# Attention's products and the combination ordered by matmul shape, and routing's small VectorE steps traced as three runs

## The chip, the cores and the metric

The kernel runs on one core of one Trainium2 chip. The metric is the device time of one execution in microseconds (us); lower is better. Three runs of the kernel before took 4184.38, 4184.52 and 4186.29 us, so its median is 4184.52 us. The engines are named as in the profile: PE is TensorE (PEld its weight loads), DVE is VectorE, ACT is ScalarE, POOL is GpSimd, and SP is the engine whose queue issues most of the DMAs.

## What is computed

The input x holds 4 images of 384 channels and 32 x 32 points, in fp32. Everything stays in fp32. Cut to what matters:

```python
# layer 0: a selective scan (a state space model) over 4 directions
dt = softplus(dts + bias); h = h * exp(dt * A) + (dt * u) * B; y = sum over 16 states of h * C
x  = x + gelu(layernorm(y0 + y1 + y2 + y3))
# layer 1: attention in a window, then a mixture of experts
t = tokens(x)                                   # per image 1024 tokens of 384
q, k, v = split(ln(t) @ qkv_w + qkv_b)          # 6 heads of 64
att = where(causal and distance <= 64, q @ k.T / 8, -inf)
t = t + (softmax(att) @ v) * gate @ proj_w + proj_b
probs = softmax(ln(t) @ gate_w + gate_b)        # 4 experts, the best 2 of them kept
t = t + sum over the 2 experts of weight * (gelu(ln(t) @ w1[e] + b1[e]) @ w2[e] + b2[e])
```

Because a token attends to itself and to at most 64 tokens before it, a tile of 128 tokens needs the 128 keys of its own and the last 64 of the tile before. The first tile of an image needs its own alone.

## The kernel before

**The order of the work** is not written by hand. Every stage is a Python generator that yields one operation at a time, and a planner, `Machine` (L211), keeps a clock for each engine. It knows an estimated cost for each operation (`Engine.ask`, L154) and takes from the waiting operations the one that can start first, corrected by a bias (`EARLY`, -6, for what feeds others; `LATER`, +6, for the experts and the combination). The order in which the planner takes the operations is the order in which each engine executes them, and the engines then wait for each other by semaphores alone. So an estimate of a cost changes no work, but it can change the order everywhere behind it. `Engine.all` (L143) takes a list of calls as one operation: they stand together in the engine's order, and nothing is placed among them. The planner also decides which of two engines does certain steps: `copy` (L557) gives a copy to DVE or ACT, and `scan` gives the multiplication by C to POOL or DVE (`on_pool`, L853).

**The scan.** The work is cut into 768 slots: 4 images, 4 directions, 12 blocks and 4 groups of states. For each slot ACT makes the decays `dA`, POOL multiplies `z <- dts, bc` (`times_b`, L804), DVE runs the scan over 1024 steps (`scan`, L846), then DVE or POOL multiplies by C, and PE folds the states together (`fold_y`, L876, the tile `ps_y`). Seven buffers `z` are in use. A fold gives its two back, so a fold that is late on PE can hold up POOL.

**Attention** (`tokens`, L953) starts for an image when its scan is done, while the scan of the next image goes on. It takes the image in 8 tiles of 128 tokens, up to three of them in progress, with one at a time in the core of attention. For each tile it does the following steps on PE, with copies and sums on the other engines between them:
- It makes q and k by 9 matmuls each (`ps_qk`). The keys of a head pair lie in 192 columns of the tile `k`: 64 old ones first, then the 128 new ones. A copy brings the old ones from the tile before.
- It makes v (`ps_v`).
- It makes the scores (`ps_s`, L1061). One matmul for each head has 64 rows, which are the head's channels, and 192 columns. DVE adds the mask and finds the maximum, and ACT takes the exponential with its sum.
- It turns the probabilities (`ps_p`, L1094), for three pairs of heads. For each head there is a transpose of the 128 new columns and, in tiles with old keys, a matmul by the identity that turns the 64 old columns onto partitions 64 to 127. Its weights have 64 columns.
- It multiplies by v (`ps_o`, L1115). For each head there is a matmul over 128 rows, the new keys, and in tiles with old keys one over 64 rows, which adds to it. The two kinds alternate. DVE then scales the result by the sums (`o <- ps_o, sums`).
- It projects (`ps_pr`), normalises, and finds the logits of the experts (`ps_xt`, with 4 columns).

**Routing** (`route`, L1196) computes for the 1024 tokens of an image the weights of the two experts and the place of each token in the lists of the experts. These are some 65 DVE steps on small tiles, with one exponential on ACT and three small matmuls on PE among them. Each step is yielded on its own. Then the tokens are scattered in DRAM by indirect DMAs.

**The experts** (`experts`, L1304) take 19 blocks of 128 tokens for each image. A block needs 36 hidden matmuls (`ps_hid`, 128 columns) and 12 output matmuls (`y_ff`, 384 columns), and 8 loads of 576 KB of weights. The experts of one image follow its routing, and PE does them between the folds and the attention of the images after it.

**The combination** (`combine`, L1396) gathers for each tile of 128 tokens the outputs of its two experts, weighs and adds them (ACT, then DVE), and turns the sum with matmuls by the identity. Onto each of three column groups it adds the biases `b2`, by a matmul over 4 rows (`ps_c`, L1421). These two kinds alternate too.

A fp32 matmul is two instructions on PE in the profile, one for each pass, and a transpose is one.

Of the kernel before, what the change touches and what calls it, by code (L numbers as in the profile page):

```python
# [17 lines left out]
P = 128  # L18
# [111 lines left out]
class Engine:  # L130
# [23 lines left out]
    def ask(self, op, a, k):  # L154
# [222 lines left out]
def conv_attn_hybrid(  # L377
# [11 lines left out]
    def const_load(src, shape, name):  # L389
# [57 lines left out]
    nc.gpsimd.affine_select(  # L447
        mask, mask, pattern=[[1, KW]], compare_op=ALU.is_ge, fill=NEG,
        base=0, channel_multiplier=-1,
# [503 lines left out]
    def tokens(b):  # L953
# [18 lines left out]
        def tile(a):  # L972
# [32 lines left out]
            for n, (w, dst) in enumerate(  # L1005
                ((wq, q[:, :D].rearrange("p (t l) -> p t l", t=T)), (wk, kv[:, :, WIN:]))
            ):
# [39 lines left out]

            lo = 0 if a else WIN
            yield lambda: len(core) < CORES
# [5 lines left out]
            def score(hps, j):  # L1055
# [3 lines left out]
                for n, hp in enumerate(hps):  # L1059
                    mm.matmul(  # L1060
                        ps[:, n * KW + lo : (n + 1) * KW],  # L1061
                        q[r, ts(hp, P)], k[r, hp * KW + lo : (hp + 1) * KW],
                        start=True, stop=True,
                    )
                yield from pe.all(mm)
                for n, hp in enumerate(hps):
                    h = 2 * hp + j
                    c = slice(n * KW + lo, (n + 1) * KW)
                    yield from dve.tensor_tensor_reduce(
                        s[hps[0] + j][:, c], ps[:, c], mask[:, lo:], 1.0, NEG,  # L1070
                        ALU.add, ALU.max, mx[:, 0, h : h + 1],
# [7 lines left out]
            for hp in range(T):  # L1079
                for j in range(2):  # L1080
                    h = 2 * hp + j
                    sj = s[hp // 2 * 2 + j][:, hp % 2 * KW + lo : (hp % 2 + 1) * KW]
                    yield from act.activation(
# [6 lines left out]
            def turn(hp):  # L1090
# [105 lines left out]
    def route(b):  # L1196
# [22 lines left out]
        yield from dve.reciprocal(r, rr)  # L1219
        yield from dve.tensor_tensor(pp, pp, bcast_last(r, NE), ALU.mult)  # L1220
        yield from dve.tensor_copy(p, pp)

        yield from dve.memset(cmp, 0.0)
        for e in range(NE):
            if e > 0:
                yield from dve.tensor_tensor(
                    cmp[:, :, e, :e], p[:, :, :e], bcast_last(pp[:, :, e], e), ALU.is_ge
                )
            if e < NE - 1:
                yield from dve.tensor_tensor(  # L1230
                    cmp[:, :, e, e + 1 :], p[:, :, e + 1 :], bcast_last(pp[:, :, e], NE - 1 - e),
                    ALU.is_gt,
                )
        sel = rp.tile([P, NT, NE], F32, tag="sel", name="sel2", bufs=1)
        yield from dve.tensor_reduce(rank, cmp, AX.X, ALU.add)
        yield from dve.tensor_scalar(sel, rank, 2.0, None, ALU.is_lt)
        yield from dve.tensor_tensor(pp, pp, sel, ALU.mult)
        yield from dve.tensor_reduce(rr, pp, AX.X, ALU.add)
        yield from dve.tensor_scalar(rr, rr, 1e-9, None, ALU.add)
        yield from dve.reciprocal(r, rr)  # L1240
        yield from dve.tensor_tensor(p, pp, bcast_last(r, NE), ALU.mult)

        accs = rp.tile([P, NT + 1, NE], F32, tag="acc", name="acc", bufs=1)
        yield from dve.memset(acc[:, 0, :], 0.0)
        for a in range(NT):
            yield from dve.tensor_tensor(acc[:, a + 1, :], acc[:, a, :], sel[:, a, :], ALU.add)
        yield from dve.tensor_copy(accs, acc)
# [4 lines left out]
        yield from pe.all(mm)  # L1254
        nb = rp.tile([P, NE], F32, tag="nb", name="nb")
        yield from dve.tensor_tensor(full, bcast_last(cn[:, NT, :], NT), bcast(count_p, NE), ALU.is_gt)
        yield from dve.tensor_reduce(nb, full, AX.X, ALU.add)

        yield from dve.tensor_copy(cum[:, :1], nb[:, :1])
        for e in range(1, NE):  # L1260
            yield from dve.tensor_tensor(
                cum[:, e : e + 1], cum[:, e - 1 : e], nb[:, e : e + 1], ALU.add
            )
        yield from dve.tensor_tensor(nb, cum, nb, ALU.subtract)
        slot = rp.tile([P, NT, NE], F32, tag="slot", name="slot", bufs=1)
        yield from dve.scalar_tensor_tensor(
            slot, bcast(nb, NT), float(P), cn[:, :NT, :], ALU.mult, ALU.add
        )

        eid = rp.tile([P, MB], mybir.dt.int32, tag="eid", name="eid")  # L1270
        yield from dve.tensor_tensor(
            past, bcast_last(count, NE - 1), bcast(cum[:, : NE - 1], MB), ALU.is_ge
        )
        yield from dve.tensor_reduce(eid_f, past, AX.X, ALU.add)
        yield from dve.tensor_copy(eid, eid_f)

# [3 lines left out]
        for n, far in enumerate((65536.0, -65536.0)):  # L1280
            yield from dve.tensor_scalar(big, sel, -far, far, ALU.mult, ALU.add)
            yield from dve.tensor_tensor(big, big, slot, ALU.add)
            yield from dve.tensor_reduce(place[:, n, :], big, AX.X, ALU.max if n else ALU.min)
            yield from dve.tensor_tensor(big, big, bcast_last(place[:, n, :], NE), ALU.is_equal)
            yield from dve.tensor_tensor(big, big, p, ALU.mult)
            yield from dve.tensor_reduce(gate[:, n, :], big, AX.X, ALU.add)
        yield from dve.tensor_copy(idx, place)
        banks.give(ps)
# [107 lines left out]
    def combine(b):  # L1396
# [3 lines left out]
        def one(a):  # L1400
# [115 lines left out]
```

## Time and profile before

| | |
|---|---|
| median of 3 runs | 4184.52 us (4184.38 to 4186.29) |
| the profiled execution | 4192.68 us, of which its span is 4190.3 us |
| mean granted TensorE clock | 0.796 |
| busy: PE / DVE / POOL / ACT | 3169.3 / 2882.8 / 2844.5 / 2403.3 us |
| product with v, `ps_o` | 720 passes, 128 rows: 342 ns mean, 64 rows: 359 ns mean |
| turned probabilities, `ps_p` | 192 transposes and 336 passes, 104.9 us busy |
| combination, `ps_c` | 384 passes, 97.8 us busy |
| last fold of the scan / start of the last combination | about 3231 us / about 4131 us |

The profile is one execution. Busy times are sums over an engine's instructions, and they say little on their own: what counts is which engine the others wait for in a stage. [...] The granted clock is the share of full speed that the throttle allows TensorE. It is 1.0 or 0.5 at any moment, and a mean in a table.

### The profile page before, as it was taken

The numbers are of one execution on the slowest core, as the hardware profiler recorded it, in microseconds if no ns is written. First come the engines' busy times: TensorE is split into PE (matmuls) and PEld (weight loads), VectorE is DVE, ScalarE is ACT, GpSimd is POOL, SyncE is SP. The second block draws the span as 40 slices with busy tenths as digits, with TensorE's granted clock in tenths as the row PEclk, the third lists the DMA queues.
The fourth block names the chain that finished last, engine by engine and source line by source line (L and its number), as shares of the span: only waits on it lengthen the run. The fifth ranks groups of instructions, "written<-read, shape, count | busy, mean of one in ns | idle before, by whom it ended". The sixth has DMA issues, their size and how long they took to land. (4 is left out here: it accounts for less than half of the span.)

```text
span 4190.3 us, 49613 instructions
## 1 busy us (share of the span) xinstructions
PE 3169.3 (76%) x16030; PEld 1930.3 (46%) x16030; DVE 2882.8 (69%) x3068; ACT 2403.3 (57%) x3952; POOL 2844.5 (68%) x1484
## 2 busy tenths in 40 slices
PE   3454454477774797777888776878899999999997
PEld 1000000044541464444545443444467788787885
DVE  2999999988888888888778899888876222201001
ACT  3555465566664788877677777776677343322221
POOL 1999889988887898989876898999887011011001
PEclk8555565577765898887779887877799999999997
DMA  5566564534346989554569875554589555798995
GB/s 202 204 232 229 190 232 139 182 108 157 103 148 211 341 303 340 187 192 147 165 222 328 307 276 205 198 189 147 185 277 345 191 185 167 247 355 298 312 317 164
DMA packets 368572, 935.12 MB, mean 223 GB/s; under 512 B 48373, under 2 KB 160121, under 8 KB 368313
## 3 DMA queue, kind: packets, MB, share of 16 engines
q1 hardware_dynamic: 360120, 906.79, 62.4%
q0 software_dynamic: 8192, 25.17, 1.7%
q8 instruction: 127, 2.08, 0.2%
q14 instruction: 133, 1.08, 0.1%
HBM read 786.39 MB, written 164.30 MB: 227 GB/s over the span
## 5 line engine op out<-in xcount | busy, mean ns | idle before, releaser
L141 POOL TENSOR_TENSOR z<-dts,bc 128x1024 f32<-128x1024 f32 x768 | 1791.4, 2357 | 233.8 <-PE ps_y L152 155.8
L152 PE MATMUL ps_y<-z,fold 128*32 128x512 f32 x3072 | 732.7, 800 | 531.3 <-POOL z L141 269.2
L141 ACT ACTIVATE dA<-dts,a 128x1024 f32<-128x1024 f32 x768 | 850.7, 1115 | 493.8 <-DVE z L141 485.7
L141 DVE TENSOR_TENSOR_SCAN dA<-dA,z 128x1024 f32<-128x1024 f32 x398 | 910.5, 2288 | 101.5 <-ACT dA L141 94.0
L141 POOL TENSOR_TENSOR z<-z,bc 128x1024 f32<-128x1024 f32 x370 | 867.4, 2355 | 128.6 <-DVE z L141 118.7
L141 DVE TENSOR_TENSOR_SCAN z<-dA,z 128x1024 f32<-128x1024 f32 x370 | 832.0, 2276 | 25.5 <-ACT dA L141 24.3
L152 PEld LDWEIGHTS ps_hid<-xbt,w_sb 128*128 128x128 f32 x5472 | 688.7, 203 | 137.0 <-issue 32.3
L152 PE MATMUL ps_hid<-xbt,w_sb 128*128 128x128 f32 x5472 | 710.5, 288 | 44.1 <-ACT dt L141 17.5
L152 PE MATMUL y_ff<-w_sb,hs 128*128 128x384 f32 x1824 | 663.8, 502 | 16.4 <-ACT hs L141 8.1
L141 ACT ACTIVATE hs<-ps_hid,bb 128x128 f32<-128x128 f32 x912 | 271.2, 367 | 486.5 <-PE ps_hid L152 390.9
L152 PEld LDWEIGHTS ps_y<-z,fold 128*32 128x32 f32 x3072 | 93.6, 123 | 953.0 <-POOL z L141 461.8
L141 DVE TENSOR_TENSOR z<-dA,bc 128x1024 f32<-128x1024 f32 x398 | 486.1, 1221 | 12.9
L141 ACT ACT_TABLE_LOAD x368 | 472.1, 1283 | 22.7 <-PE ps_g L152 7.7
L152 PEld LDWEIGHTS y_ff<-w_sb,hs 128*128 128x128 f32 x1824 | 330.9, 194 | 237.8 <-issue 42.9
L141 POOL DMA_INDIRECT cb<-ysdr,idx x64 | 61.8, 966 | 499.2 <-DMA cb<-t2dr 265.4
L141 DVE COPY xbt<-ps_xb 128x384 f32<-128x384 f32 x36 | 20.0, 557 | 384.4 <-PE ps_xb L152 384.3
L152 POOL TENSOR_TENSOR rn<-rn,half 128x1 f32<-128x1 f32 x96 | 52.4, 546 | 279.4 <-DVE rn L152 273.7
L152 PE MATMUL ps_o<-v,pt 128*128 128x64 f32 x720 | 163.0, 350 | 18.5 <-DVE tt L141 6.5
L141 POOL DMA_INDIRECT xsdr<-tks,idx x64 | 64.1, 1001 | 152.2 <-DMA xsdr<-tks,idx 97.2
L152 PEld LDWEIGHTS ps_o<-v,pt 128*128 128x128 f32 x720 | 133.0, 233 | 57.8 <-ACT dt L141 8.2
L152 PE MATMUL ps_p<-ident,s 128*128 128x128 f32 (+1 forms) x528 | 104.9, 328 | 47.7 <-ACT dt L141 21.1
L152 PE MATMUL ps_dt<-xd,dtw_sb 12*128 12x512 f32 x192 | 97.5, 858 | 43.9 <-ACT dt L141 19.4
(188 smaller groups left out, 3314.7 us busy)
## 6 DMA issues: line engine op xcount, KB each, us to landing
w_sb<-wl SPq DMA_DIRECT2D x608, 576.0 KB
dts<-dtr SPq DMA_DIRECT2D x384, 512.0 KB
bc<-xdr SPq DMA_DIRECT2D x128, 512.0 KB
ub<-udr SPq DMA_DIRECT2D x48, 512.0 KB
dtr<-e SPq DMA_DIRECT2D x48, 512.0 KB
dtr<-dt SPq DMA_DIRECT2D x48, 512.0 KB
yp<-ydr SPq DMA_DIRECT2D x96, 256.0 KB
ydr<-yp SPq DMA_DIRECT2D x96, 256.0 KB
```

Source lines behind the costliest of these rows:

```text
L141: return getattr(self.real, op)(*a, **k)
L152: getattr(self.real, op)(*a, **k)
```

## The change

There are four parts.

1. The keys are laid out with the 128 new ones first and the 64 old ones behind. Masks, copies and slices follow. The mask is built by three selections on POOL instead of two.
2. The turned probabilities come from transposes alone. The old keys are turned by a transpose of the last 128 columns (64 new, 64 old) of the 192, of which partitions 64 to 127 are used.
3. In the product with v all heads' 128-row matmuls come first, then all 64-row ones. One accumulation covers the bank: the first matmul starts it, and the last ends it. The combination does the same with its identity matmuls and its 4-row ones.
4. Routing's DVE steps are handed to the planner as three lists, one up to the exponential, one up to the matmuls and one behind them, instead of one by one. And the planner's estimate of a matmul has a floor of 122 columns instead of 90.

```diff
-            cost = max(n, 90) * (0.00088 if op == "transpose" else 0.00176)
+            cost = max(n, 122) * (0.00088 if op == "transpose" else 0.00176)
...
     nc.gpsimd.affine_select(
-        mask, mask, pattern=[[-1, KW]], compare_op=ALU.is_ge, fill=NEG,
-        base=WIN, channel_multiplier=1,
+        mask[:, :P], mask[:, :P], pattern=[[-1, P]], compare_op=ALU.is_ge, fill=NEG,
+        base=0, channel_multiplier=1,
     )
...
-                yield from copy(kv[:, :, :WIN], old.rearrange("p (t l) -> p t l", t=T)[:, :, P:])
+                yield from copy(kv[:, :, P:], old.rearrange("p (t l) -> p t l", t=T)[:, :, P - WIN : P])
...
                 for j in range(2):
-                    mm.transpose(ps[:, ts(j, P)], s[base + j][:, c0 + WIN : c0 + KW], ident)
+                    mm.transpose(ps[:, ts(j, P)], s[base + j][:, c0 : c0 + P], ident)
                 for j in range(2 if a else 0):
-                    mm.matmul(
-                        ps[WIN:, ts(2 + j, P)], s[base + j][:, c0 : c0 + WIN], ident,
-                        start=True, stop=True,
-                    )
+                    mm.transpose(ps[:, ts(2 + j, P)], s[base + j][:, c0 + KW - P : c0 + KW], ident)
...
-            for hp, pt in sorted(pts.items()):
-                for j in range(2):
-                    hc = slice((2 * hp + j) * HD, (2 * hp + j + 1) * HD)
-                    mm.matmul(po[:, hc], pt[:, ts(j, P)], v[:, hc], start=True, stop=not a)
-                    if a:
-                        mm.matmul(
-                            po[:, hc], pt[WIN:, ts(2 + j, P)], vts[a - 1][WIN:, hc],
-                            start=False, stop=True,
-                        )
+            for old in (False, True) if a else (False,):
+                for hp, pt in sorted(pts.items()):
+                    for j in range(2):
+                        hc = slice((2 * hp + j) * HD, (2 * hp + j + 1) * HD)
+                        if old:
+                            lhs, rhs = pt[WIN:, ts(2 + j, P)], vts[a - 1][WIN:, hc]
+                        else:
+                            lhs, rhs = pt[:, ts(j, P)], v[:, hc]
+                        last = len(mm) == (2 if a else 1) * HEADS - 1
+                        mm.matmul(po[:, hc], lhs, rhs, start=not mm, stop=last)
...
-        yield from dve.tensor_reduce(r, p, AX.X, ALU.max)
-        yield from dve.tensor_tensor(pp, p, bcast_last(r, NE), ALU.subtract)
+        mm = Calls()
+        mm.tensor_reduce(r, p, AX.X, ALU.max)
+        mm.tensor_tensor(pp, p, bcast_last(r, NE), ALU.subtract)
+        yield from dve.all(mm)
         yield from act.activation(pp, pp, AF.Exp)
-        yield from dve.tensor_reduce(rr, pp, AX.X, ALU.add)
+        mm = Calls()
+        mm.tensor_reduce(rr, pp, AX.X, ALU.add)
...
             for t in range(T):
                 c = ts(t, P)
-                mm.matmul(ps[:, c], gs[0][:, c], ident, start=True, stop=False)
-                mm.matmul(ps[:, c], b2_sb[:, c], gt[:NE, :P], start=False, stop=True)
+                mm.matmul(ps[:, c], gs[0][:, c], ident, start=t == 0, stop=False)
+            for t in range(T):
+                c = ts(t, P)
+                mm.matmul(ps[:, c], b2_sb[:, c], gt[:NE, :P], start=False, stop=t == T - 1)
```

More of the change, by code (lines that the diff above doesn't have):

```diff
@@ L443, in conv_attn_hybrid @@
     nc.gpsimd.affine_select(
-        mask, mask, pattern=[[-1, KW]], compare_op=ALU.is_ge, fill=NEG,
-        base=WIN, channel_multiplier=1,
+        mask[:, :P], mask[:, :P], pattern=[[-1, P]], compare_op=ALU.is_ge, fill=NEG,
+        base=0, channel_multiplier=1,
     )
     nc.gpsimd.affine_select(
-        mask, mask, pattern=[[1, KW]], compare_op=ALU.is_ge, fill=NEG,
+        mask[:, :P], mask[:, :P], pattern=[[1, P]], compare_op=ALU.is_ge, fill=NEG,
+        base=WIN, channel_multiplier=-1,
+    )
+    nc.gpsimd.affine_select(
+        mask[:, P:], mask[:, P:], pattern=[[1, WIN]], compare_op=ALU.is_ge, fill=NEG,
         base=0, channel_multiplier=-1,
@@ L1005, in tile @@
             for n, (w, dst) in enumerate(
-                ((wq, q[:, :D].rearrange("p (t l) -> p t l", t=T)), (wk, kv[:, :, WIN:]))
+                ((wq, q[:, :D].rearrange("p (t l) -> p t l", t=T)), (wk, kv[:, :, :P]))
             ):
@@ L1046, in tile @@
             vts[a] = v
-            lo = 0 if a else WIN
+            n_keys = KW if a else P
             yield lambda: len(core) < CORES
@@ L1060, in score @@
                     mm.matmul(
-                        ps[:, n * KW + lo : (n + 1) * KW],
-                        q[r, ts(hp, P)], k[r, hp * KW + lo : (hp + 1) * KW],
+                        ps[:, n * KW : n * KW + n_keys],
+                        q[r, ts(hp, P)], k[r, hp * KW : hp * KW + n_keys],
                         start=True, stop=True,
@@ L1067, in score @@
                     h = 2 * hp + j
-                    c = slice(n * KW + lo, (n + 1) * KW)
+                    c = slice(n * KW, n * KW + n_keys)
                     yield from dve.tensor_tensor_reduce(
-                        s[hps[0] + j][:, c], ps[:, c], mask[:, lo:], 1.0, NEG,
+                        s[hps[0] + j][:, c], ps[:, c], mask[:, :n_keys], 1.0, NEG,
                         ALU.add, ALU.max, mx[:, 0, h : h + 1],
@@ L1081, in tile @@
                     h = 2 * hp + j
-                    sj = s[hp // 2 * 2 + j][:, hp % 2 * KW + lo : (hp % 2 + 1) * KW]
+                    sj = s[hp // 2 * 2 + j][:, hp % 2 * KW : hp % 2 * KW + n_keys]
                     yield from act.activation(
@@ L1214, in route @@
         r = rp.tile([P, NT], F32, tag="r", name="r")
-        yield from dve.tensor_reduce(r, p, AX.X, ALU.max)
-        yield from dve.tensor_tensor(pp, p, bcast_last(r, NE), ALU.subtract)
+        mm = Calls()
+        mm.tensor_reduce(r, p, AX.X, ALU.max)
+        mm.tensor_tensor(pp, p, bcast_last(r, NE), ALU.subtract)
+        yield from dve.all(mm)
         yield from act.activation(pp, pp, AF.Exp)
-        yield from dve.tensor_reduce(rr, pp, AX.X, ALU.add)
[L1219 to L1223, printed above, removed]
+        mm = Calls()
+        mm.tensor_reduce(rr, pp, AX.X, ALU.add)
+        mm.reciprocal(r, rr)
+        mm.tensor_tensor(pp, pp, bcast_last(r, NE), ALU.mult)
+        mm.tensor_copy(p, pp)
+        mm.memset(cmp, 0.0)
         for e in range(NE):
             if e > 0:
-                yield from dve.tensor_tensor(
+                mm.tensor_tensor(
                     cmp[:, :, e, :e], p[:, :, :e], bcast_last(pp[:, :, e], e), ALU.is_ge
@@ L1229, in route @@
             if e < NE - 1:
-                yield from dve.tensor_tensor(
+                mm.tensor_tensor(
                     cmp[:, :, e, e + 1 :], p[:, :, e + 1 :], bcast_last(pp[:, :, e], NE - 1 - e),
@@ L1234, in route @@
         sel = rp.tile([P, NT, NE], F32, tag="sel", name="sel2", bufs=1)
[L1235 to L1241, printed above, removed]
+        mm.tensor_reduce(rank, cmp, AX.X, ALU.add)
+        mm.tensor_scalar(sel, rank, 2.0, None, ALU.is_lt)
+        mm.tensor_tensor(pp, pp, sel, ALU.mult)
+        mm.tensor_reduce(rr, pp, AX.X, ALU.add)
+        mm.tensor_scalar(rr, rr, 1e-9, None, ALU.add)
+        mm.reciprocal(r, rr)
+        mm.tensor_tensor(p, pp, bcast_last(r, NE), ALU.mult)
         accs = rp.tile([P, NT + 1, NE], F32, tag="acc", name="acc", bufs=1)
-        yield from dve.memset(acc[:, 0, :], 0.0)
+        mm.memset(acc[:, 0, :], 0.0)
         for a in range(NT):
-            yield from dve.tensor_tensor(acc[:, a + 1, :], acc[:, a, :], sel[:, a, :], ALU.add)
-        yield from dve.tensor_copy(accs, acc)
+            mm.tensor_tensor(acc[:, a + 1, :], acc[:, a, :], sel[:, a, :], ALU.add)
+        mm.tensor_copy(accs, acc)
+        yield from dve.all(mm)
         mm = Calls()
@@ L1254, in route @@
         yield from pe.all(mm)
+        mm = Calls()
         nb = rp.tile([P, NE], F32, tag="nb", name="nb")
-        yield from dve.tensor_tensor(full, bcast_last(cn[:, NT, :], NT), bcast(count_p, NE), ALU.is_gt)
-        yield from dve.tensor_reduce(nb, full, AX.X, ALU.add)
-        yield from dve.tensor_copy(cum[:, :1], nb[:, :1])
+        mm.tensor_tensor(full, bcast_last(cn[:, NT, :], NT), bcast(count_p, NE), ALU.is_gt)
+        mm.tensor_reduce(nb, full, AX.X, ALU.add)
+        mm.tensor_copy(cum[:, :1], nb[:, :1])
         for e in range(1, NE):
-            yield from dve.tensor_tensor(
+            mm.tensor_tensor(
                 cum[:, e : e + 1], cum[:, e - 1 : e], nb[:, e : e + 1], ALU.add
             )
-        yield from dve.tensor_tensor(nb, cum, nb, ALU.subtract)
+        mm.tensor_tensor(nb, cum, nb, ALU.subtract)
         slot = rp.tile([P, NT, NE], F32, tag="slot", name="slot", bufs=1)
-        yield from dve.scalar_tensor_tensor(
+        mm.scalar_tensor_tensor(
             slot, bcast(nb, NT), float(P), cn[:, :NT, :], ALU.mult, ALU.add
@@ L1270, in route @@
         eid = rp.tile([P, MB], mybir.dt.int32, tag="eid", name="eid")
-        yield from dve.tensor_tensor(
+        mm.tensor_tensor(
             past, bcast_last(count, NE - 1), bcast(cum[:, : NE - 1], MB), ALU.is_ge
         )
-        yield from dve.tensor_reduce(eid_f, past, AX.X, ALU.add)
-        yield from dve.tensor_copy(eid, eid_f)
+        mm.tensor_reduce(eid_f, past, AX.X, ALU.add)
+        mm.tensor_copy(eid, eid_f)
         place = rp.tile([P, 2, NT], F32, tag="place", name="place", bufs=1)
@@ L1280, in route @@
         for n, far in enumerate((65536.0, -65536.0)):
[L1281 to L1287, printed above, removed]
+            mm.tensor_scalar(big, sel, -far, far, ALU.mult, ALU.add)
+            mm.tensor_tensor(big, big, slot, ALU.add)
+            mm.tensor_reduce(place[:, n, :], big, AX.X, ALU.max if n else ALU.min)
+            mm.tensor_tensor(big, big, bcast_last(place[:, n, :], NE), ALU.is_equal)
+            mm.tensor_tensor(big, big, p, ALU.mult)
+            mm.tensor_reduce(gate[:, n, :], big, AX.X, ALU.add)
+        mm.tensor_copy(idx, place)
+        yield from dve.all(mm)
         banks.give(ps)
```

## The prediction

> **What bounds the kernel now.** I read the busy table by stage first, then the waits inside the long stage, then single stretches of the timeline. By stage (us from the span's start; busy us and instructions of each engine, granted TensorE clock, DMA share, GB/s):
>
> ```profile
> core 0: us, PE busy (x) PEld busy (x) DVE busy (x) ACT busy (x) POOL busy (x), PEclk, DMA share, GB/s
> 100.00:880.00 780.00, 392.29 (x1144) 76.56 (x1144) 746.16 (x541) 417.92 (x489) 730.96 (x329) 0.59 0.57 199
> 880.00:3231.00 2351.00, 1824.88 (x9332) 1110.54 (x9331) 1975.16 (x2038) 1680.02 (x2614) 2020.45 (x1018) 0.80 0.64 222
> 3231.00:3640.00 409.00, 399.77 (x2464) 320.57 (x2460) 99.39 (x350) 152.37 (x424) 37.38 (x68) 0.96 0.59 190
> 3640.00:4131.00 491.00, 484.43 (x2931) 385.86 (x2930) 30.47 (x73) 118.83 (x383) 30.63 (x32) 0.99 0.90 317
> 4131.00:4190.30 59.30, 36.69 (x102) 24.22 (x102) 9.98 (x20) 5.12 (x11) 15.12 (x16) 0.52 0.39 110
> ```
>
> Up to 880 only the scan runs, DVE 96% busy; the change touches nothing there. From 880 to 3231, the last fold, the scan shares the core with attention and experts: DVE 84% and POOL 86% busy, so their idle time is what can be won ("middle stage"). From 3231 TensorE never rests ("tail"): there each TensorE microsecond is a microsecond of the end. After 4131 only the last batch's combination is left, at half clock. Waits of 880 to 3231 (us in total, times, longest):
>
> ```profile
> POOL z L141 <- PE ps_y L152: 154.1, 55, 9.1
> DVE o L141 <- PE ps_o L152: 69.4, 22, 6.3
> ```
>
> DVE, in the stage that it sets, stands 69 us before the product of attention and V. One such place, in the timeline:
>
> ```profile
> 961.13 7.47 PE L152 MATMUL ps_o<-v,pt 128*128 128x64 f32 x24 [4.20 <-ACT yl L141]
> 968.64 0.56 DVE L141 TENSOR_TENSOR o<-ps_o,sums 128x384 f32<-128x384 f32 x1 [3.92 <-PE ps_o L152]
> 971.26 2.35 POOL L141 TENSOR_TENSOR z<-dts,bc 128x1024 f32<-128x1024 f32 x1 [3.99 <-PE ps_y L152]
> ```
>
> TensorE takes 7.47 us, DVE idles 3.92 for it, and the fold queued behind it lets POOL idle 3.99.
>
> **What a change of shape costs.** Each fp32 matmul is two passes, a transpose one. Starts on TensorE, at full clock but for the pair at 3608:
>
> ```profile
> 3314.93 1.45 PE L152 MATMUL ps_o<-v,pt 128*128 128x64 f32 x12
> 3316.21 1.00 PE L152 MATMUL ps_hid<-xbt,w_sb 128*128 128x128 f32 x7
> 3441.77 4.33 PE L152 MATMUL ps_o<-v,pt 128*128 128x64 f32 x24
> 3446.03 0.55 PE L152 MATMUL ps_t<-ident,tt 128*128 128x128 f32 x3
> 3598.08 0.49 PE L152 MATMUL ps_t<-ident,tt 128*128 128x128 f32 x3
> 3598.41 0.96 PE L152 MATMUL ps_p<-ident,s 128*128 128x128 f32 x6
> 3599.30 0.55 PE L152 MATMUL ps_xb<-ident,xb 128*128 128x128 f32 x3
> 3608.38 1.44 PE L152 MATMUL ps_xt<-gw_sb,xlt 128*128 128x4 f32 x6
> 3609.68 1.63 PE L152 MATMUL ps_hid<-xbt,w_sb 128*128 128x128 f32 x6
> ...
> 3811.88 0.39 PE L152 MATMUL ps_c<-ident,cb 128*128 128x128 f32 x2
> ...
> 3814.27 0.94 PE L152 MATMUL ps_hid<-xbt,w_sb 128*128 128x128 f32 x6
> ```
>
> A batch's first tile, all of 128 rows, starts 12 passes in 1.28 us. A later tile, two of 128 rows and two of 64 in turn, takes 4.26 for 24. So one of its 12 changes costs (4.26 - 2.56) / 12 = 0.14 us.
>
> **Product with V** (L1115): 12 passes of 128 rows, one change, 12 of 64, one change: 2.56 + 0.28 = 2.84, saving 1.42 per later tile. The trace has no run of 64-row, 64-column passes. The nearest row of 64 rows, the scores with 192 columns, starts passes 0.163 apart; at that price the saving is 0.8. The Trainium skill ("TensorE: Matmul & The Clock Gate", LDWEIGHTS) says that loading weights takes time by their columns, not their rows; both kinds have 128, 107 ns as its estimate, against 107 here (1.28 / 12). I take 0.107, since a pass of 64 columns streams a third of the 192; the other end stays for the range. At half clock a pass is 1.30 / 6 = 0.217, so 7.47 holds 5.2 of passes and 0.19 per change: new 5.6, saving 1.9.
>
> **Turning the probabilities** (L1095): two transposes and two two-pass products of 64 output rows become four transposes. Now 0.89, plus 0.05 by which the next group (0.38 for three instead of 0.33) is late; new 4 x 0.11 = 0.44. Saves 0.5 per pair of heads, three pairs a tile; at half clock a group at 2119 took 1.66 against 4 x 0.217, saving 0.8.
>
> **Combination** (L1421): 2.39 with six changes. Same-shape passes 1.28, so 0.185 a change; new 1.28 + 0.37 = 1.65, saving 0.74. In the last combination the chain shows
>
> ```profile
> 4152.76 4.42 PE ps_c L152 x12
> ```
>
> at half clock: 2.6 of passes, 0.30 per change, new 3.2, saving 1.2.
>
> **Sum of the tail.** Seven later tiles x (1.42 + 1.5) = 20.4, and 1 for two product runs at half clock; 16 combinations x 0.74 = 11.8; the last eight x 1.2 = 9.6, which fits because the gathers, 5 us from issue to use, still land within a tile's 5.9 - 1.2. Together 43. Against it stands the order: in the changed kernel's instruction order 33.75 hidden blocks and 33 output blocks precede the last fold, before 35.25 and 35. So 1.5 x 72 passes x 0.112 = 12.1 and 2 x 24 x 0.323 = 15.5 move into the tail: +27.6. Net -15.
>
> **Sum of the middle stage.** 21 later tiles, about half at each clock: 1.66 each, 35 us. DVE idles 69.4 / 22 = 3.2 at each, at the end of the run, so all 35 come out of DVE's idle time. DVE waits only 5 us for the turned probabilities here (26.4 in all, 21.2 in the tail): 3. POOL is as full as DVE and can be next to hold, so of 38 I take three quarters: -29; ends -75 (POOL's waits for folds shrink too) and +8.
>
> A rule that speaks against it: the same page (PE-mode transpose) says that transposes don't count as busy for the clock gate. Transposes of probabilities go from 192 to 360 and 336 matmul passes go. By the rule the attention stretches could sink to half clock, the product then costs 5.6 against 5.85 now (the mean of the 21 runs), the middle wins some 5, and the time is 4165. By the rows the tail holds 0.96 to 0.99 with transposes among blocks, and folds and blocks stand between attention's pieces. I take the rows.
>
> **At nothing.** Routing's some 65 DVE steps of 0.06 to 0.3 us already stand nearly together (2246.8 to 2263.1 with two large ones between; the changed order has two or three too); in the first batch they take 1271.5 to 1299 and may take 10 less, hidden while TensorE has folds; without that cover, 10. The mask's third select (0.34 each, at 4 us, first score at 865): covered by POOL's wait for the first load. The plan puts 378 instead of 370 second multiplications on POOL: DVE -8 x 1.22 = -10, POOL +8 x 2.36 = +19; cancelled by balance, within the range.
>
> Sum: -15 - 29 = -44. The profiled execution, 4192.7 (span 4190.3 and 2.4 around it), becomes 4149; against the median of the runs, 4184.5, it is 4140.
>
> **Rivals.**
> - Hidden anyway: POOL (2020 busy of 2351) holds the middle stage, folds wait for their own passes, only the tail's -15 stays: 4170. For it: POOL is the fuller engine. Against: DVE's 69 us.
> - More than that: L177 prices 64-column matmuls by 122 columns instead of 90, 12 x 0.158 = 1.9 becoming 2.6 against the 4.3 to 7.5 that the trace shows now and 2.8 to 5.6 then. The plan fits, folds are no longer late, and 60 of POOL's 154 us go too, three quarters of them won: 4095.
> - Half effect: the 64-row passes cost 0.163. Then 0.67 less is saved by each run, 7 x 0.67 in the tail and 21 x 0.67 x 3/4 in the middle, 15 together: 4155. For it: no such run stands in the trace. Against: load time by columns.
> - Slower: by the second routing the changed order has put 16.75 blocks on TensorE, before 15.5, at nearly the same place in the scan (after the 134th and the 133rd of 192 fold groups). 1.25 blocks of 16.1 us at full and 31 at half clock stand in front of folds between 1300 and 2256. If all of it (20 to 39) reaches POOL and swallows what DVE wins: 4184.5 - 15 + 35 = 4205. It decides from 23 us on. Against: the same order has fewer blocks by the end of the stage.
>
> **How the numbers follow.** Forecast 0.45 (own range 4118 to 4160), hidden 0.22, more 0.20, half effect 0.04, slower 0.09. A tenth below and a tenth above give 4090 to 4177. Within 0.2% (8 us, what a measurement of this kernel tells from no change) lies the upper edge of "hidden" and the lower edge of "slower": 0.04. Faster 0.88, slower 0.08.
>
> **What would show it.** Later tiles' product runs of 24 passes in 2.8 us at full clock; 360 turning instructions of 0.11; combinations of 1.65, in the last chain 3.2 instead of 4.42; DVE's wait for ps_o in the middle near 35; last fold near 3200; from the last fold to the end about 945 instead of 959. Wrong if POOL's wait for ps_y grows, if the granted clock of the middle falls below 0.75, or if the last fold stays at 3231.

## The result, and the profile after

| | before | after |
|---|---|---|
| median of 4 runs each, us | 4184.45 (4183.37 to 4186.29) | 4113.22 (4111.46 to 4114.65) |
| ratio, 95% interval | | 0.9829 (0.9812 to 0.9846) |
| span of the profiled execution, us | 4190.3 | 4111.9 |
| last fold of the scan, us from the start | 3231 | 3169 |
| from the last fold to the end, us | 959 | 943 |

The changed kernel is 71 us faster. The forecast was 44; the time lies outside the forecast's own range (4118 to 4160) and inside the wide one (4090 to 4177). Where the time came from is seen in the stages. These are the stretches of the kernel after, in the columns of the prediction's first fence (microseconds, then busy time and instructions of PE, its weight loads, DVE, ACT and POOL, then granted clock, DMA share and GB/s):

```profile
100.00:880.00 780.00, 405.42 (x1161) 79.64 (x1162) 745.12 (x542) 421.98 (x493) 736.72 (x332) 0.58 0.56 199
880.00:3169.00 2289.00, 1707.17 (x9034) 1043.79 (x9032) 1967.92 (x2019) 1689.77 (x2616) 2039.59 (x1027) 0.80 0.64 224
3169.00:3525.00 356.00, 344.02 (x2264) 284.00 (x2263) 97.50 (x350) 145.74 (x399) 34.67 (x65) 0.97 0.60 195
3525.00:4060.00 535.00, 526.81 (x3230) 421.93 (x3229) 32.80 (x78) 130.50 (x421) 30.71 (x32) 0.99 0.90 320
4060.00:4111.90 51.90, 27.20 (x102) 21.91 (x102) 10.01 (x21) 5.23 (x11) 15.17 (x16) 0.53 0.44 126
```

The scan's opening is as before. The middle stage ends 62 us earlier, with DVE and POOL doing the same work (1968 and 2040 us, before 1975 and 2020) in less time: both idle less. The tail is 16 us shorter, of which 7 lie in the last batch's combination (51.9 us against 59.3).

The waits of 880 to 3169, in the kernel after (us in total, times, longest):

```profile
POOL z L141 <- PE ps_y L152: 81.2, 49, 7.9
...
DVE o L141 <- PE ps_o L152: 8.2, 10, 2.7
```

DVE stood 69.4 us before the product of attention and V, and now 8.2. POOL stood 154.1 us before folds, and now 81.2. The prediction had the first near 35 and left the second to a rival. Not all of this comes from the matmuls, as E1 and E2 show below.

Passes overlap in the profile: those of the product before last 342 and 359 ns in the mean, yet 24 of them start within 4.26 us. So starts are compared, not durations. The matmuls themselves, from three places of the tail in the timeline of the kernel after (start, duration, number of matmul instructions):

```profile
3295.86 2.93 PE L152 MATMUL ps_o<-v,pt 128*128 128x64 f32 x24
3298.71 0.50 PE L152 MATMUL ps_xt<-gw_sb,xlt 128*128 128x4 f32 x3
...
3374.58 1.47 PE L152 MATMUL ps_p<-ident,s 128*128 128x128 f32 x12
3375.89 0.83 PE L152 MATMUL ps_hid<-xbt,w_sb 128*128 128x128 f32 x6
...
3396.33 0.83 PE L152 MATMUL ps_c<-ident,cb 128*128 128x128 f32 x6
3397.10 0.93 PE L152 MATMUL ps_c<-cb,b_sb 4*128 4x128 f32 x6
3397.96 0.71 PE L152 MATMUL ps_hid<-xbt,w_sb 128*128 128x128 f32 x4
```

From start to start, a product of 24 passes takes 3298.71 - 3295.86 = 2.85 us. Twelve turning transposes, which are three pairs of heads, take 1.31, or 0.44 for a pair. A combination takes 1.63. The last two combinations, in the chain that ended last:

```profile
4100.45 3.24 PE ps_c L152 x12
...
4104.94 3.21 PE ps_c L152 x12
```

The forecast had 2.84, 0.44, 1.65 and 3.2. Other product runs of the tail take up to 2.96, and those at half clock about 5.5, for which the forecast had 5.6.

### The profile page after: what moved, and what is told of

Read it like the earlier page. It is cut to its first block, busy times and chain, and to the rows that moved or that the text cites. A ratio compares the mean times of both kernels' runs of the same rounds, so it can differ in the third digit from the quotient of the medians.

```text
span 4111.9 us, 49282 instructions
## 1 busy us (share of the span) xinstructions
PE 3040.7 (74%) x15850; PEld 1863.6 (45%) x15850; DVE 2875.1 (70%) x3057; ACT 2421.9 (59%) x3972; POOL 2865.5 (70%) x1493
## 5 line engine op out<-in xcount | busy, mean ns | idle before, releaser
L152 PE MATMUL ps_y<-z,fold 128*32 128x512 f32 x3072 | 745.1, 811 | 554.9 <-POOL z L141 269.5
L141 DVE TENSOR_TENSOR_SCAN dA<-dA,z 128x1024 f32<-128x1024 f32 x390 | 891.9, 2287 | 96.8 <-ACT dA L141 79.5
L141 POOL TENSOR_TENSOR z<-z,bc 128x1024 f32<-128x1024 f32 x378 | 887.9, 2360 | 95.7 <-DVE z L141 89.4
L141 DVE TENSOR_TENSOR_SCAN z<-dA,z 128x1024 f32<-128x1024 f32 x378 | 850.5, 2275 | 44.2 <-ACT dA L141 42.8
L141 DVE TENSOR_TENSOR z<-dA,bc 128x1024 f32<-128x1024 f32 x390 | 476.1, 1221 | 13.2
L152 PE MATMUL ps_o<-v,pt 128*128 128x64 f32 (+1 forms) x720 | 112.7, 320 | 21.9 <-ACT dt L141 10.1
L152 PEld LDWEIGHTS ps_o<-v,pt 128*128 128x128 f32 (+1 forms) x720 | 107.6, 232 | 34.8 <-ACT dt L141 15.4
L141 ACT COPY dt<-ps_sp 128x512 f32<-128x512 f32 x96 | 56.1, 585 | 110.9 <-DVE e L141 110.7
```

The costliest lines, as they stand in the source:

```text
L141: return getattr(self.real, op)(*a, **k)
L152: getattr(self.real, op)(*a, **k)
```

## The experiments

Two theories came out of this result. In the first, called "passes" in the expectations, the matmuls by shape do the work, each worth the time of its own passes, and what the middle won beyond the forecast came from the new order. In the second, "plan", the order does more than the matmuls. A third came up on the way: "clock", that the alternating matmuls cost more than their own time because TensorE falls to half clock around them.

To separate matmuls and order, `Engine.all` gets an amount that it adds to the cost it tells the planner, so that a group keeps the price it had in the other kernel. In E1, E3, E4, E5, E6 and E12 every engine has its instructions in the order of before, and in E2 in the order of after; only the matmuls inside the groups differ.

| run | what it is | median us | ratio to before, 95% interval | last fold | to the end |
|---|---|---|---|---|---|
| E1 | new matmuls, order of before | 4071.5 | 0.9717 (0.9695 to 0.9738) | 3166 | 915 |
| E2 | old matmuls, order of after | 4239.7 | 1.0131 (1.0114 to 1.0148) | 3238 | 996 |
| E3 | combination by shape alone | 4162.3 | 0.9944 (0.9928 to 0.9961) | 3224 | 936 |
| E4 | product with v by shape alone | 4094.2 | 0.9785 (0.9769 to 0.9801) | 3153 | 940 |
| E5 | turning by transposes alone | 4181.2 | 0.9979 (0.9971 to 0.9988) | 3231 | 950 |
| E6 | E4 with 6 matmuls that nothing reads in each product | 4130.3 | 0.9871 (0.9837 to 0.9905) | 3172 | 952 |
| E12 | E4 with 8 matmuls that nothing reads in each product | 4138.4 | 0.9881 (0.9864 to 0.9897) | 3188 | 949 |
| E7 | after, floor 90 | 4086.1 | 0.9765 (0.9737 to 0.9794) | 3113 | 966 |
| E8 | after, routing step by step | 4112.0 | 0.9818 (0.9790 to 0.9846) | 3166 | 955 |
| E9 | after, floor 106 | 4126.9 | 0.9848 (0.9832 to 0.9865) | 3184 | 951 |
| E10 | after, floor 140 | 4103.7 | 0.9796 (0.9779 to 0.9812) | 3111 | 992 |
| E11 | after, floor 90, routing step by step | 4089.5 | 0.9760 (0.9743 to 0.9776) | 3156 | 933 |

The kernel before had medians of 4185.5 beside E1 to E4, 4191.2 beside E5 to E8, 4189.8 beside E9 to E11 and 4187.5 beside E12, so the ratios are what compares. 0.01 is 42 us.

### Matmuls and order apart: E1 and E2

E1 has all of the changed kernel's matmuls, and its planner is told the old costs:

```diff
-    def all(self, calls):
+    def all(self, calls, extra=0.0):
...
-        whole.work = sum(o.work for o in asked)
+        whole.cost += extra
+        whole.work = sum(o.work for o in asked) + extra
...
-            cost = max(n, 122) * (0.00088 if op == "transpose" else 0.00176)
+            cost = max(n, 90) * (0.00088 if op == "transpose" else 0.00176)
...
-                yield from pe.all(mm)
+                yield from pe.all(mm, 0.22528 if a else 0.0)
```

Routing's steps are single in it, as before. E2 is the reverse: the changed kernel with the old matmuls of all three places, and `pe.all(mm, -0.22528 if a else 0.0)` in the turning group.

> The matmuls of the changed kernel in the order of the kernel before: routing's steps one by one, the floor of 90 columns, and the turned probabilities charged to the planner as before, so that every engine has its instructions in exactly the order of before. Theory 'passes' (the shorter runs on TensorE give the gain, and the other order is neutral, because the blocks that it moves into the tail leave the middle stage): tail -43 (attention 22, combinations 21), middle -29 to -38, so 4103 to 4113 us, the last fold near 3195 and 905 to 915 us from there to the end. Theory 'plan' (the new order is what wins the middle stage): tail -43, middle -10 at most, so 4131 us or more, the last fold at 3220 or later.

> The matmuls of before (alternating products with v, turned old keys as two-pass products with 64 columns, alternating combination) in exactly the order of the changed kernel: routing in three runs, floor of 122, and the turned probabilities charged as the transposes are. Theory 'passes': 4176 to 4192 us, no measurable difference from before: the tail gets 27 us longer by the moved blocks, the middle as much shorter. Theory 'plan': the middle keeps most of its 62 us, and the time is 4150 us or less.

E1 came 32 us below the range of "passes". E1 in stages, and then E2 (columns as above):

```profile
880.00:3166.00 2286.00, 1734.81 (x9193) 1070.03 (x9195) 1969.73 (x2036) 1676.21 (x2609) 2018.60 (x1017) 0.81 0.65 228
3166.00:4080.00 914.00, 874.35 (x5456) 710.47 (x5456) 139.67 (x441) 276.83 (x820) 83.25 (x116) 0.96 0.76 262
```

```profile
880.00:3238.00 2358.00, 1790.61 (x9142) 1085.72 (x9144) 1967.81 (x2019) 1688.01 (x2611) 2036.70 (x1027) 0.79 0.62 218
3238.00:4233.00 995.00, 952.97 (x5638) 752.42 (x5634) 140.72 (x447) 281.68 (x831) 80.85 (x114) 0.95 0.73 248
```

Both expectations of E2 fell. The order of after gains nothing and is not neutral: it costs 55 us with the old matmuls and, after against E1, 42 us with the new. The matmuls are then worth more than the whole change: 114 us in the old order, 126 in the new. By the last fold, the order made 3 us (E1 to after) and 7 us (before to E2); the rest is in the tail, where PE has 5638 matmul instructions in E2 against 5497 in before, and 5596 in after against 5456 in E1. These are 140 more with either kind of matmul, and the tail is 36 and 28 us longer for them. The middle stage lost that work and got no shorter. E1's profiled execution was the slowest of its four (4083.3; the others 4057.9 to 4076.2), so its stages add up to some 12 us more than its median.

The waits of E1 from 880 to 3166:

```profile
POOL z L141 <- PE ps_y L153: 103.7, 44, 9.5
...
DVE o L141 <- PE ps_o L153: 35.9, 19, 3.7
```

So the new matmuls alone bring DVE's wait to 35.9, which is what the prediction said. The rest of the way to 8.2 is the order's: E2, with the old matmuls, has 36.1 as well. But the last fold of the changed kernel comes no earlier than E1's, so these 28 us of wait were not won as time.

### One shape at a time: E3, E4 and E5

Each is the kernel before with one of the three edits of the diff, the product's and the combination's as printed there. E5 takes the whole key layout with it, and the charge of E1.

> The kernel before with the combination's matmuls by shape and nothing else; the order of the instructions is that of before. Theory 'passes': 16 combinations under a full TensorE save 0.77 us each, the last eight 1.2 each at half clock, 4184 - 22 = 4162 us (4158 to 4166); the last stretch, from the first to the last combination of the last batch, falls from 44 to about 35 us. Rival: the gathers set the pace of the last combination, which then gives nothing, 4171 us.

> The kernel before with the product with v by shape and nothing else; the order of the instructions is that of before. Theory 'passes': 7 later tiles in the tail save 1.5 us each, -11; in the middle stage DVE's wait for ps_o falls from 69 to about 35 us and three quarters of it are won, so -11 - 26 = 4147 us (4138 to 4156). Rival 'hidden': POOL holds the middle stage, which does not get shorter, 4173 us.

> The kernel before with the new layout of the keys and the turned probabilities by transposes alone, charged to the planner as before, so that the order is that of before; products with v and combination alternate as before. Theory 'passes' as forecast: 21 groups in the tail save 0.5 us each, -11; the middle stage wins 2 to 5, so 4170 us (4164 to 4175). Rival 'hidden' (the two runs with the product alone and with all three leave nothing for it, 4185 - 23 - 91 = 4071, which is what all three gave): 4180 to 4190 us, since the pieces stand between waits for the copies of the probabilities.

E3 came where "passes" put it, 23 us below before, and its tail is 23 us shorter. E5 won 9 us by its ratio, and its tail is 9 shorter; the middle, where 3 were forecast, shows none. By its ratio it would be 4176 us, between the ranges of its two theories and nearer to "passes". E4 won 90, more than twice what was expected. The three together make 0.0056 + 0.0215 + 0.0021 = 0.0292, and E1 has 0.0283: the parts add up, and the product is three quarters of the whole. The three tails together are 51 us shorter and E1's is 44, so a single part is known to some 7 us.

The waits of E4 from 880 to 3150:

```profile
POOL z L141 <- PE ps_y L152: 100.3, 44, 8.3
...
DVE o L141 <- PE ps_o L152: 26.8, 15, 3.7
```

Of the product's own wait, 69.4 - 26.8 = 43 us went. The mean product run of a later tile fell from 5.60 to 3.58 us (from its first start to the start of the next matmul, 28 runs, both clocks), which is 2.0 x 21 = 42 us in the middle. But the last fold came 78 us earlier, and POOL's wait for folds, which are other matmuls, fell by 54 (by 5 in E3). So about half of what the product's edit won does not stand in its own passes.

### The product's time given back: E6 and E12

Both are E4 with matmuls by the identity into columns of the bank that nothing reads, between the 128-row and the 64-row matmuls. They fill the time that the edit saved, in one shape and without a pause, and the planner is told nothing of them:

```diff
+            fill = 6 if a else 0
             for old in (False, True) if a else (False,):
+                for n in range(fill if old else 0):
+                    mm.matmul(po[:, D:HB], pts[n % T][:, :P], ident, start=False, stop=False)
...
-            yield from pe.all(mm)
+            yield from pe.all(mm, -0.22528 * fill)
```

E12 has 8 in place of 6.

> The product with v by shape as in the run with the product alone, with six matmuls by the identity into unused columns of the bank ahead of the 64-row ones, so that TensorE spends about the old time there (4.2 us at full clock, 8 at half, before 4.3 and 7.4) but without changes of shape; the order is that of before. It adds work whose result nothing reads. Theory 'time' (the product's shorter time on TensorE is the whole gain): 4175 to 4195 us, about as before. Theory 'clock' (the array idles at each change of shape, and the clock gate takes that for idleness, so that other matmuls run at half clock too): a third or more of the 91 us stays, 4155 us or less, and the time at half clock in the middle stage, 935 us before and 823 with the product alone, stays below 880.

> As the run with six matmuls of fill, with eight. With six the mean product run of a later tile took 5.14 us against 5.60 before, so some of its 0.987 could still be time saved; with eight it should take 5.6 to 5.8, as before or more. The added work is read by nobody. Theory 'clock': most of what was left stays, ratio to before 0.985 to 0.993, the time at half clock in the middle stage below 850 us. Theory 'time': the ratio returns to 0.998 or above.

The mean product run is 5.14 us in E6 and 5.45 in E12, before 5.60. So E12 gives nearly all of it back, though less than the 5.6 that was expected; 0.15 x 21 = 3 us can still be time saved. Both runs came where "clock" put them. Yet 0.0119 of E4's 0.0215 stays, 55%, and 60% in E6. In the waits of E12 from 880 to 3188, the two parts stand apart:

```profile
POOL z L141 <- PE ps_y L153: 108.7, 44, 7.7
...
DVE o L141 <- PE ps_o L153: 63.7, 22, 6.4
```

DVE's wait for the product is back (63.7, before 69.4). POOL's wait for the folds is not (108.7, before 154.1). The granted clock differs with it. This is the tile `ps_o` from 880 to 3150, with PE's, its loads' and DVE's busy time on it, and then the granted clock of the whole stretch, DMA share and GB/s. First before:

```profile
880.00:3150.00 2270.00, 127.14 (x540) 103.37 (x540) 13.38 (x24) 0.79 0.62 217
```

Then E4, E6 and E12:

```profile
880.00:3150.00 2270.00, 82.62 (x528) 78.79 (x528) 13.27 (x24) 0.82 0.65 229
```

```profile
880.00:3150.00 2270.00, 111.88 (x780) 106.83 (x780) 13.38 (x24) 0.83 0.64 226
```

```profile
880.00:3150.00 2270.00, 122.92 (x870) 117.81 (x869) 13.37 (x24) 0.82 0.64 224
```

With nearly as much busy time on the product as before (123 of 127 us), the clock of the stage stays at E4's 0.82. Added up from the clock's records, TensorE is at half clock in the middle stage for 935 us in before, 905 in E3 and 990 in E5, all with the alternating product and one order. In that order with the product by shape it is 885 in E1, 823 in E4, 775 in E6 and 795 in E12. The middle stage of E3 differs from that of before in eight combinations alone, so one profile scatters by some 30 us.

The mean clock of every run is on record, too. As the clock is 1.0 or 0.5, twice the share that is missing, times the span, is the time at half clock in the whole execution:

| in the order of before | product | runs | us at half clock, mean (range) |
|---|---|---|---|
| before, beside E1 to E4 | alternating | 7 | 1715 (1672 to 1750) |
| E3 | alternating | 4 | 1704 (1664 to 1723) |
| before, beside E5 and E6 | alternating | 23 | 1723 (1679 to 1752) |
| E5 | alternating | 20 | 1757 (1727 to 1806) |
| before, beside E12 | alternating | 7 | 1726 (1700 to 1748) |
| E1 | by shape | 4 | 1609 (1582 to 1641) |
| E4 | by shape | 4 | 1609 (1591 to 1621) |
| E6 | by shape and filled | 4 | 1565 (1538 to 1599) |
| E12 | by shape and filled | 4 | 1570 (1548 to 1588) |

Alternating and by shape don't overlap here. Another order moves the clock as well: E2 has 1784, and the changed kernel 1677.

The same can be counted run by run, over the later tiles' products of all profiles:

| product runs of 24 passes | began at full clock, ended at half | began at half, ended at full |
|---|---|---|
| alternating (before, E2, E3, E5) | 45 of 80 | 0 of 32 |
| by shape (after, E1, E4, E7 to E11) | 22 of 152 | 11 of 72 |
| by shape and filled (E6, E12) | 1 of 42 | 13 of 14 |

So the alternating run tends to end at half clock, and the matmuls behind it start there. Where the clock stays up, these are shorter: after 880, the folds are busy for 421 us in before and 403 in E12, and PE's matmuls other than folds, product and turning for 1216 and 1184. Of these 50 us E3 shows 19 too (414 and 1204), mostly by scatter. Shown is that the clock differs with the shape of the run, that the gain outlasts the run's length, and that it is then in the folds' wait. That a faster PE between the products is the link is argued from these, since no run sets the clock by itself. The scatter between executions of one program speaks for a weaker link: over 112 recorded runs, each compared with others of its own program, 10 us more at half clock go with 1 us more time. But there the half clock may fall where nothing waits for PE. And the filled runs don't only stop lowering the clock, they raise it, so the 55 and 60% are not a measure of that part in E4.

### What in the new order costs: E7 to E11

E7, E9 and E10 are the changed kernel with another floor in the planner's estimate:

```diff
-            cost = max(n, 122) * (0.00088 if op == "transpose" else 0.00176)
+            cost = max(n, 90) * (0.00088 if op == "transpose" else 0.00176)
```

E9 has 106 and E10 140. E8 has the floor of 122, and routing's steps yielded one by one. E11 has both the floor of 90 and single steps, so that of the change it holds the shapes alone, at the planner's price for each.

> The changed kernel with the planner's floor of 90 columns, as before; all its matmuls and routing's three runs stay. The order of the changed kernel costs 42 to 54 us (4113 against 4071 with the new matmuls, 4240 against 4185 with the old ones). Theory 'floor': the floor does it, and this run comes to 4071 to 4085 us. Theory 'routing': routing's runs do it, and this run stays at 4105 to 4120. Theory 'chance' (any disturbance of the plan moves the order, and the sum by some 20 us either way): anything between 4060 and 4140.

> The changed kernel with routing's steps given to the planner one by one, as before; the floor of 122 and all matmuls stay. Theory 'floor': 4105 to 4120 us. Theory 'routing': 4071 to 4085 us. Theory 'chance': anything between 4060 and 4140, and not the complement of the run with the floor of 90.

> The changed kernel with the planner's floor at 106 columns, between 90 (ratio to before 0.9765) and 122 (0.9829). Theory 'systematic' (a higher price for the 64-column matmuls makes the plan worse step by step): between the two, 4090 to 4110 us. Theory 'chance' (each price is another order, and orders scatter): outside of these, 4060 to 4088 or above 4116 us.

> The changed kernel with the floor at 140 columns. Theory 'systematic': worse than at 122, 4118 to 4145 us. Theory 'chance': as likely better as worse, 4060 to 4140 us; only 31 hidden blocks precede the last fold, before 33.75, which by the price of a block in the tail is 16.1 x 2.7 = 43 us against it unless the middle stage is shorter by as much.

> The changed kernel with the floor of 90 and routing's steps one by one: it differs from the run of the new matmuls in the old order by one thing, that the turned probabilities are charged to the planner as the transposes that they are (0.45 us a pair of heads instead of 0.68), which makes another order. Theory 'systematic': the truer price is no worse, 4065 to 4080 us. Theory 'chance': 4085 to 4110 us, like the changed kernel with the floor of 90 (4086) and unlike the old order (4071).

E7 came 1 us above the range of "floor", and E8 in it; E9, E10 and E11 came where "chance" put them. Routing's three runs are worth nothing that these runs can tell: E8 has 0.9818 and the changed kernel 0.9829, E11 has 0.9760 and E7 0.9765, with intervals that overlap. The floor of 122 costs about 27 us against 90. But there is no direction in it: 90, 106, 122 and 140 give 0.9765, 0.9848, 0.9829 and 0.9796. Each gives another order, and the orders scatter over 35 us. E11 differs from E1 in the price of the turning alone, which is truer in E11, and is 18 us slower. Nor is it work moved into the tail alone: E7 is faster than the changed kernel with a tail that is 23 us longer (966), since its last fold comes 56 us earlier, and E10 has the longest tail, 992. The clock orders them in part. By the means of all runs, E1 has 1609 us of half clock, E7 1646, E11 1676, E10 1643, the changed kernel 1677, E8 1713 and E9 1721, for 4072, 4086, 4090, 4104, 4113, 4112 and 4127 us. The fastest has the least and the slowest the most, but E10 falls out of line, and in E8 one run of four makes 25 of the 1713. Whether the clock makes an order slow, or its waits lower the clock, is not shown. All of these orders are slower than that of before, which E1 has, though E7's interval touches E1's. What makes that one better wasn't found.

## Why the prediction was right or wrong

**The prices of a change of shape: right.** Turning and combinations came within 0.04 us, and the product within 0.12. The disputed 64-row pass is 0.112 us from the next in the trace of after, not 0.163: that rival (half effect) fell. The rule of the Trainium skill on weight loads ("TensorE: Matmul & The Clock Gate", LDWEIGHTS), time by columns and not by rows, agrees with this: the 128-row passes of the same runs start 0.112 apart too. The 0.107 was 5% low.

**The tail: right in sum.** Its saving was put at 43, and E1's tail is 44 shorter than that of before. The moved blocks were put at +27.6, and the tail of after is 28 longer than E1's. The net of -16 against -15 is thus no balance of two errors. E3's 23 of the tail answers to the combination's 21.4. For turning, 9 (E5) stand against 10.5. For the product it is 19 (E4) against 10.9, off by about the 7 us to which single parts are known.

**The middle stage: the step that failed.** "All 35 come out of DVE's idle time", with three quarters of that and of the turning's 3 won, gave -29. Measured were -62, and -65 in the order of before. The mechanism was right as far as it went: DVE's wait for the product fell to the 35 that was said (35.9 in E1). The term mis-sized is the product's, on two counts. It was taken as its own passes at the clocks of before, 1.66 a run, while the runs were also more often at full clock and came out 2.0 shorter. And its worth was counted to the engine that waits for it alone. E4's middle is 78 shorter, 42 by its own runs, and E12 shows that a gain stays when the run is long again. The prediction bounded the gain at -75 and named POOL's waits as the reason, which is where it was found, but gave it too little weight.

**The clock: weighed at the wrong place.** I asked whether more transposes would lower the clock. E5 has them, at 990 us of half clock in the middle against 935 and 905 for the same stage in before and E3. One profile can't tell that from the scatter, but the recorded clocks can: E5's 20 runs have a mean of 0.790, the 23 of before beside them 0.794, which is 34 us more at half clock. That is the direction of the rule (the same page of the skill, PE-mode transpose). Whether it is because transposes don't count, or because TensorE has less to do, is not separated, and the effect was small: the time still went down by 9. The alternating product, at which the clock falls, was priced by its length alone. The trace of before had it to see: 20 of its 28 product runs began at full clock, 10 of these ended at half, and none went up.

**The order: half right.** The change was taken as paying in the tail only, with the early blocks (rival "slower") as a risk. In the tail that held. But the prediction took the order for given with the change, and it is the larger loss: 42 us by the medians, more than half of the result. The estimate's floor makes some 27 of it (E7), and routing's runs none; the truer price of the turning makes about the rest (18, E11 against E1).

**Luck in the sum.** The matmuls were forecast at 43 + 29 = 72 us and gave 114, and the order was forecast to cost 27.6 and cost 42. The two misses have opposite signs, so the total is nearer to its forecast than the matmuls' part.

**Rivals.** "Hidden anyway" fell, as POOL did not hold the stage. "More than that" came nearest in the time (4095 against 4113) and in POOL's wait, which fell by 73 where 60 was said (by 50 in E1, with the plan of before). Its reason fell: a price nearer to the trace gave a slower plan (E7 against after), and E4 has most of the effect with the plan of before. "Slower" needed 23 us in the middle; the order cost 3 to 7 there.

**At nothing.** Routing was right (E8).

**What stays open.** Two explanations of how the alternating run lowers the clock are left: it may be by its pauses at each change of shape, or by the small part of the array that 64 rows and 64 columns use for so long. How much of E4's gain outside its own passes is the clock, and how much is a chain of waits that shifts, is not separated. And no run tells why one order is better than another.

A better version came out of the study. E1, with the new matmuls in the order of before, takes 4071.5 us, 0.9717 (0.9695 to 0.9738) of before, and is about 42 us faster than the changed kernel.

## What to carry to other kernels

Sort matmuls by the rows and columns that they use. Price the sorting first by the changes of shape, from start to start, and then look at the clock granted around such runs, since the work beside them may gain too. Where a planner orders the instructions, try a new matmul with the old order held, before its price is corrected: a truer estimate is another draw of the order, and here the draws lay 35 us apart.

## What was not expected of the hardware

At full clock the passes of one shape start 0.112 us apart. Where the shapes alternate, a pass starts 0.205 behind one of the other shape and 0.160 behind the first pass of its own matmul, which is the 0.14 for each change. The cause is the change and not the adding to columns just written: the way back to 128 rows, which starts new columns, costs 0.202, and in the sorted product the one change left still costs 0.205 and 0.160, about twelve passes behind the matmuls that wrote its columns. Nor is it that each head had an accumulation of its own, as the first tiles of before have that too, at 0.112. Such a run of 4.3 us also tends to end at half clock: 56% of those that began at full did, against 14% of those by shape. They last 1.5 times as long, which alone doesn't make the fourfold, and none of 32 that began at half rose. Six or eight dense matmuls of 128 rows and 128 columns in the same run turned that over: 13 of 14 rose. A price per matmul doesn't hold this, since part of the gain is in the work that comes next.
